# A third sorted set at the end of a four-layer kernel: batches 12 to 14 take one expert each row, batch 15 both; small constants on SP's queue

## The chip, the cores and the metric

The kernel runs on one core of a Trainium2 chip. The metric is the device time of one execution in microseconds (us), the median of several runs; less is better. The core has a matrix engine (PE, with its weight loads shown apart as PEld), a vector engine (DVE), an activation engine (ACT), a general engine (POOL), and SP, which does nothing but issue transfers. Transfers (DMAs) are issued by SP, ACT or POOL, each into a queue of its own, and carried by 16 DMA engines that all queues share. Each engine works through its own list of instructions in order.

## The reference

Sixteen batches (B = 16) of 112 rows (S) with 256 features (D), each with a context of 375 rows (SK), pass through four layers, each added to its input x. "ln" is a layer norm without weights.

```python
x = x + xattn0(ln(x), ctx)      # 16 heads of 64: q, k, v, softmax, Wo, bo
x = x + ffn0(ln(x))             # two experts, top-1, and a shared one
x = x + xattn1(ln(x), ctx)      # one head, no weights, rows masked
x = x + ffn1(ln(x))             # int8: scale from the largest |ln(x)| of ALL batches
```

The second layer matters here. Its gate gives each row to one of two experts; the other expert sees a row of zeros, so it gives the row a constant, `relu(b1) @ w2 + b2`:

```python
one_hot = one_hot(argmax(softmax(xf @ gate_w.T)), 2)
masked = xf[None] * one_hot.T[:, :, None]
h = relu(einsum('end,edh->enh', masked, w1) + b1[:, None])   # hidden 1024
routing_output = (einsum('enh,ehd->end', h, w2) + b2[:, None]).sum(0)
shared = relu(xf @ sw1 + sb1) @ sw2 + sb2
```

The fourth layer can't start before every batch has its third layer's result, since its scale is a maximum over all of them. All inputs are float32.

## The kernel before

**The stream.** The first layer is cut into 64 units (NU), four per batch, four heads each. `unit(u)` (L1055) writes out by hand what each engine does in unit u: the transposes of unit u-1's probabilities (`unit_T`, DVE, L432), scores and exponentials of unit u (L382, L399), the weighted sum of unit u-3 (L466), twelve small DMAs on SP that move blocks of transposed probabilities between partitions (`unit_move`, L444, tile pT), kT for unit u+1 (L296), the division of the probabilities by their sums on POOL in two halves (`divide`, L411), and v for unit u-2 (L317). Three more units drain it. Everything else is hung on units: `at(u, f)` puts a function at the unit's end (list `extra`), `mid(u, f)` puts it in its middle, after v and ahead of the second half of the divisions (L1090). Norms are chains of small steps that `pump` spreads between other instructions. Nothing is reordered by a scheduler: each engine's order is the program's order.

**The experts.** Batches 0 to 7 and 8 to 11 form two sorted sets (`SORTED`, L48). For each of their batches, `sort_gate` finds each row's expert (L537), `sort_place` its place in a buffer in DRAM, one expert's rows from the front and the other's from the back (L549), and `sort_put` scatters the rows there, an indirect DMA of POOL (L567). When a set is complete, `sort_counts` (L575) counts, and for each slot (128 or 112 rows, one more slot than the rows fill) gives the expert that the slot needs. SP reads that number into a register and loads this expert's weights, two tiles of 1 MB (`slot_weights`, L644, two buffers each), and the slot's rows (`slot_rows`, L649). PE then transposes the rows (`slot_turn`) and runs them through the one expert (`slot_run`, L724); `slot_store` writes the result back to DRAM (L732), and `sort_get` gathers each batch's rows from there, an indirect DMA of POOL (L738). `sort_add` adds them, with the constant of the other expert, and starts the next norm. Besides, `shared` (L715) runs the shared expert for two batches at once, and `Rows.run` is the loop of both: a first-layer step for each of 8 blocks of the hidden layer (L694) and a second-layer step behind it (L681).

Batches 12 to 15 are not sorted. The class `Experts` (L756) runs all their rows through the shared expert and both others, with a mask that zeroes the rows of expert 0: 24 steps (8 blocks by 3), for 12 and 13 together (224 columns), then for 14, then for 15 (112 columns each). Its lines are L800 (first layer) and L777 (second). The weights for it, 4 MB, are loaded by SP in units 61 and 62 (L1042 to L1044). Its steps are laid between the last units, the second attention of batches 8 to 11, and later between the second attention of 12 to 15 (L1106 to L1185).

**The third layer** per batch is `second_1` to `second_4` (L829 to L864): a transpose, scores against the transposed context (ctxT2, reloaded by `ctxT_again`), a softmax, a transpose, and the sum over the context (ctx_nat, reloaded by `load_ctx`, L103, 125 partitions by 3 by 256). `third_norm` and `third` prepare the fourth layer. For sorted batches the result goes to DRAM and comes back before the closing stage (L1154); for the others it stays in SBUF.

**The start.** SP and ACT load the weights of the first layer and the first contexts; POOL's queue loads the small constants (`row_to_all` L174, `small_const` L942, and others to L956) and fills the sorted buffers with zeros (L905). POOL adds the row bo to x (L336) before any division.

Of the kernel before, what the change touches and what calls it, by code (L numbers as in the profile page):

```python
# [47 lines left out]
SORTED = ((0, 8, 128), (8, 12, 112))  # L48
NSORT = SORTED[-1][1]


@with_exitstack
def tile_kernel(
# [120 lines left out]
    def row_to_all(src, name):  # L174
        t = const.tile([S, D], F32, tag=name, name=name)
        nc.gpsimd.dma_start(out=t, in_=src.partition_broadcast(S))
        return t
# [107 lines left out]
    def ctxT_again(b):  # L285
        if b < NSORT:
            t = ctxp.tile([P, DC, SK], F32, tag="ctxT_2", name=f"ctxT2_{b}", bufs=2)
        else:
            t = fin[0].tile([P, DC, SK], F32, tag="ctxT_2", name=f"ctxT2_{b}", bufs=B - NSORT)
        nc.sync.dma_start(out=t, in_=ctxT_d[b])  # L290
        ctxT2[b] = t
# [200 lines left out]
    def ffn_turn(b):  # L492
        g, i = divmod(b, GB)
        finish(("l1", b))
        if b >= B - GB:

            tiles = [
                fin[0].tile([P, DC, S], F32, tag=f"ffn_x{k}", name=f"ffn_x{k}_{b}", bufs=2)
                for k in range(2)
            ]  # L500
            ffn_in[b] = tiles
        else:
            if i == 0:
                group[g] = [
                    tmp.tile([P, DC, GT], F32, tag=f"ffn_x{k}", name=f"ffn_x{k}_{g}", bufs=1)
                    for k in range(1 if b < NSORT else 2)
                ]
            ffn_in[b] = [t[:, :, i * S : (i + 1) * S] for t in group[g]]
        transposed(ffn_in[b][0], normed["l1", b], f"x1_{b}")

    def gate_scores(b):
        pg = gen(f"pg_{b}")
        for dc in range(DC):
            nc.tensor.matmul(
                pg[:S, :2],
                ffn_in[b][0][:, dc, :],
                gw_sb[:, dc, :],
                start=(dc == 0),
                stop=(dc == DC - 1),
            )  # L520
# [12 lines left out]
    def ffn_turn_masked(b):  # L533
        transposed(ffn_in[b][1], masked[b], f"m1_{b}")
# [180 lines left out]
    def shared(g):  # L715

        acc = Rows(f"sh{g}", group[g][0], GB, big["sw1"], sb1_sb, big["sw2"]).run()
        sl = xall[:, g * GB : (g + 1) * GB, :]
        nc.vector.tensor_tensor(sl, acc[:S, :, :D], sl, ALU.add)
        for i in range(GB):  # L720
            b = g * GB + i
# [34 lines left out]
    class Experts:  # L756


        def __init__(self, bs, xT, m1T):
            self.bs, self.n, self.behind = bs, 0, deque()  # L760
            self.acc, self.columns = None, len(bs) * S
            self.masks = (xT, m1T)
            last = [expert_w["last", e] for e in range(2)]
            self.steps = []
            for k, (src, wa, ba, wb) in enumerate(
                (
                    (xT, big["sw1"], sb1_sb, big["sw2"]),
                    (m1T, last[1][0], b1_sb[:, 1, :], last[1][1]),
                    (xT, last[0][0], b1_sb[:, 0, :], last[0][1]),
                )  # L770
            ):
                self.steps += [(k, f, src, wa, ba, wb) for f in range(FC)]

        def second_layer(self, n, hT):
            _, f, _, _, _, wb = self.steps[n]
            for i in range(len(self.bs)):
                nc.tensor.matmul(  # L777
                    self.acc[:S, i, :D],
                    hT[:, i * S : (i + 1) * S],
                    wb[:, f, :],  # L780
                    start=(n == 0),
                    stop=(n == len(self.steps) - 1),
                )

        def run(self, count):
            name, c = self.bs[0], self.columns
            if self.acc is None:
                self.acc = ps_sc.tile([P, 2, 512], F32, tag="sc", name=f"acc_{name}")
            for _ in range(count):
                n = self.n  # L790
                if n == len(self.steps):
                    return
                k, f, src, wa, ba, wb = self.steps[n]
                if k == 2 and f == 0:

                    xT, m1T = self.masks
                    nc.gpsimd.tensor_tensor(xT, xT, m1T, ALU.subtract)
                ph = gen(f"ph_{name}_{n}")
                for dc in range(DC):
                    nc.tensor.matmul(  # L800
                        ph[:, :c],
# [5 lines left out]
                hT = tmp.tile([P, GT], F32, tag="hT", name=f"hT_{name}_{n}", bufs=3)[:, :c]  # L807
                if n % 2:
                    nc.vector.tensor_scalar(hT, ph[:, :c], ba[:, f : f + 1], 0.0, ALU.add, ALU.max)
                else:  # L810
                    nc.scalar.activation(hT, ph[:, :c], AF.Relu, bias=ba[:, f : f + 1])
                pump(1 + n % 2)
                self.behind.append((n, hT))
                if len(self.behind) > 2:
                    self.second_layer(*self.behind.popleft())
                self.n += 1

        def add(self):
            self.run(len(self.steps))
            while self.behind:  # L820
                self.second_layer(*self.behind.popleft())
            for i, b in enumerate(self.bs):
                nc.vector.tensor_tensor(xs[b], self.acc[:S, i, :D], xs[b], ALU.add)
                chain(("l2", b), norm([b], "l2"))
# [49 lines left out]
    def third(bs):  # L874

        finish(("l3", bs[0]))
        for b in bs:
            if b < NSORT:
# [15 lines left out]
    class Sorted:  # L894
        def __init__(self, first, last, slot):
# [8 lines left out]

            nc.gpsimd.dma_start(  # L905
                out=self.x.rearrange("(s p) d -> p s d", p=slot),
                in_=idle[:slot, :D].unsqueeze(1).to_broadcast([slot, self.slots, D]),
            )
# [20 lines left out]

    sorts = [Sorted(*a) for a in SORTED]  # L930
# [9 lines left out]
    x3T_d = dram.tile([NSORT, P, DC, S], F32, tag="x3T_d", name="x3T_d")  # L940

    def small_const(src, name, dtype=F32):  # L942
        t = const.tile(list(src.shape), dtype, tag=name, name=name)
        nc.gpsimd.dma_start(out=t, in_=src)
# [6 lines left out]
    nc.gpsimd.dma_start(out=b2r_sb[:2], in_=b2_rows)  # L951
    nc.gpsimd.dma_start(out=b2r_sb[2:], in_=sb2_row)
# [3 lines left out]
    nc.gpsimd.dma_start(out=wi8_sb, in_=wi8_t.rearrange("(c p) n -> p c n", p=P))  # L956
# [12 lines left out]
    for b in range(B):  # L969
# [8 lines left out]
        if b >= B - GB:  # L978
            continue
        at(u0 + UN + 3, ffn_turn, b)  # L980
        if b < NSORT:
            mid(u0 + UN + 4, sort_gate, b)
            at(u0 + UN + 4, sort_place, b)
            at(u0 + UN + 5, sort_put, b)
            continue
        mid(u0 + UN + 4, gate, b)
        at(u0 + UN + 4, ffn_turn_masked, b)
# [16 lines left out]
    at(3, load_big, "sw2", sw2)  # L1004
    for e in range(2):
# [3 lines left out]
    experts = {}  # L1009
    blocks = set()  # L1010
    for g in range(NSORT // GB):

        u = (g + 1) * GU + UN
        at(u, shared, g)
        blocks.add(u)
    for s in sorts:
        u = s.last * UN + UN
        at(u, sort_counts, s)
        u += 2
# [10 lines left out]
        for b in range(s.first, s.last):  # L1030
            mid(u - 2, sort_get, b)
            at(u, load_ctx, b, True)
# [9 lines left out]
    for j, e in enumerate((1, 0)):  # L1042
        for part in range(2):
            mid(NU - 3 + j, load_expert, ("last", e), e, part)  # L1044
# [61 lines left out]
    for u in range(NU):  # L1106
        unit(u)

    g6 = NG - 2
    b0, b1 = g6 * GB, B - GB  # L1110
    first = Experts([b0, b0 + 1], *group[g6])
    first.run(2)
    for u in range(NU, NU + 3):
        unit(u, lambda: first.run(2))
        first.run(2)
# [3 lines left out]
    for b in range(b0, B):  # L1119
        load_ctx(b, True)  # L1120
        ctxT_again(b)
# [191 lines left out]
```

## Time and profile before

| | us |
|---|---|
| Median of three runs (1113.59 to 1114.34) | 1113.76 |
| The profiled execution's own time | 1112.52 |
| Its span, first instruction to last | 1110.8 |
| PE busy in the span | 1015.4 (91%) |
| DVE, ACT, POOL busy | 522.2, 457.8, 444.2 |
| Last weighted sum of the first attention (unit 63's) starts | 986.0 |
| Last expert step ends | 1078.2 |

Span and execution time differ by 1.7 us, which lies around the first and last instruction. Times in the views are microseconds from the span's start. "L466" is a line of the kernel. In a view by lines or in a timeline, "out<-in xN" gives the tiles written and read and the number of instructions; what stands in brackets is how long the engine was idle before and what ended it. "SPq" and the like are an engine's instruction queue, for SP its DMA issues. "PEclk" is the clock that the throttle granted to PE as a share of the full one. "DMA" is the mean busy share of the 16 DMA engines.

The profile shows an almost always busy PE with two kinds of exceptions: the first 40 us, and about 910 to 958 us, the last units. The closing stage after 1078.2 is a chain of latencies (batch 15's third layer, the global maximum, and the quantized product of all batches).

### The profile page before, as it was taken

The page shows a single profiled execution, that of the slowest core. Times are in us where ns is not written, and L with a number is a line of the kernel's source. Part 1 is how long each engine was busy: PE and PEld are TensorE (multiplying, and loading weights), DVE is VectorE, ACT ScalarE, POOL GpSimd, SP SyncE. Part 2 cuts the span into 40 slices and gives each one's busy share as a digit, 9 for nine tenths or more (in the row PEclk, how much of TensorE's full clock was granted, in tenths as well). Part 3 has the DMA queues.
Part 4 walks back from the last instruction along what each step waited for, and adds up shares of the span by engine and source line. Part 5 has one row for each costly group of instructions (what it writes and reads, how often), then busy time and mean ns, then how long its engine had stood idle before and what let it go on. Part 6 is the DMA issues. An engine that isn't in the chain of part 4 may idle for free. (4 is left out here: it accounts for less than half of the span.)

```text
span 1110.8 us, 17703 instructions
## 1 busy us (share of the span) xinstructions
PE 1015.4 (91%) x6021; PEld 772.1 (70%) x6021; DVE 522.2 (47%) x1304; ACT 457.8 (41%) x1241; POOL 444.2 (40%) x479
## 2 busy tenths in 40 slices
PE   7899999999999999999999997988889977799995
PEld 4576677767777776877768774676667755588774
DVE  3647535554463554344342346536535345333324
ACT  2664535653553465343441435335333444112212
POOL 5654534552544455232330326535322436113113
PEclk9899999999999999999999999989999998799997
DMA  9663312231231223175563423425645416424002
GB/s 278 164 172 94 80 39 70 74 85 34 79 88 45 64 75 84 28 205 148 159 200 101 130 66 103 124 64 144 176 127 149 147 40 210 120 81 129 1 1 67
DMA packets 142850, 117.83 MB, mean 106 GB/s; under 512 B 15190, under 2 KB 133288, under 8 KB 142760
## 3 DMA queue, kind: packets, MB, share of 16 engines
q1 hardware_dynamic: 131848, 102.51, 33.0%
q10 hardware_dynamic: 8960, 9.39, 3.0%
q0 software_dynamic: 1952, 4.81, 1.4%
q8 instruction: 48, 0.79, 0.3%
q14 instruction: 42, 0.34, 0.1%
HBM read 64.92 MB, written 13.98 MB: 71 GB/s over the span
## 5 line engine op out<-in xcount | busy, mean ns | idle before, releaser
L411 POOL TENSOR_SCALAR p<-p,rden 128x375 f32<-128x375 f32 x256 | 316.6, 1250 | 331.0 <-DVE rden L408 326.0
L399 ACT ACTIVATE p<-sc,nmax 128x375 f32<-128x375 f32 x256 | 143.2, 570 | 258.5 <-DVE nmax L390 250.1
L296 PE MATMUL pk<-ctxT,wk 128*128 128x375 f32 x512 | 195.4, 505 | 8.6 <-ACT v L328 4.0
L317 PE MATMUL pv<-wv,ctxT 128*128 128x256 f32 (+1 forms) x768 | 190.3, 384 | 7.3 <-ACT v L328 6.2
L317 PEld LDWEIGHTS pv<-wv,ctxT 128*128 128x128 f32 (+1 forms) x768 | 143.9, 189 | 59.0 <-ACT v L328 11.4
L432 DVE STREAM_TRANSPOSE blk<-p 128x384 f32<-128x384 f32 x256 | 131.7, 551 | 20.8 <-POOL p L411 17.5
L454 ACT COPY pT<-blk 32x384 f32<-32x384 f32 x256 | 130.0, 508 | 16.2 <-DVE rden L408 11.8
L296 PEld LDWEIGHTS pk<-ctxT,wk 128*128 128x128 f32 x512 | 91.8, 194 | 63.7 <-issue 13.2
L382 PE MATMUL sc<-kT,qT 64*128 64x375 f32 x512 | 103.2, 518 | 11.8 <-ACT kT L305 9.8
L390 DVE TENSOR_REDUCE nmax<-sc 128x2 f32<-128x750 f32 x128 | 112.2, 913 | 3.6 <-PE sc L382 3.5
L466 PEld LDWEIGHTS pa<-pT,v 128*64 128x64 f32 (+1 forms) x1536 | 75.7, 138 | 35.1 <-issue 18.9
L330 DVE COPY v<-pv 119x256 f32<-119x256 f32 x64 | 26.9, 421 | 144.9 <-PE pv L317 143.5
L466 PE MATMUL pa<-pT,v 128*64 128x112 f32 (+1 forms) x1536 | 90.5, 266 | 4.0 <-DVE v L330 4.0
L237 POOL TENSOR_SCALAR var_l<-mv_l 112x1 f32<-112x1 f32 (+1 forms) x56 | 13.1, 233 | 166.4 <-DVE mv_l L234 139.9
L382 PEld LDWEIGHTS sc<-kT,qT 64*128 64x128 f32 x512 | 44.5, 190 | 46.2 <-ACT kT L305 14.3
L305 ACT COPY kT<-pk 128x375 f32<-128x375 f32 x128 | 61.4, 480 | 16.7 <-PE pk L296 16.1
L486 PE MATMUL po<-wo,oT 128*112 128x256 f32 x256 | 59.6, 387 | 1.3 <-ACT v L328 1.3
L353 PE MATMUL pq<-xT,wq 128*128 128x224 f32 x256 | 54.9, 357 | 4.5 <-ACT v L328 3.9
L486 PEld LDWEIGHTS po<-wo,oT 128*112 128x112 f32 x256 | 46.4, 182 | 12.7 <-ACT v L328 2.2
L353 PEld LDWEIGHTS pq<-xT,wq 128*128 128x128 f32 x256 | 46.7, 190 | 7.9 <-ACT v L328 6.0
L399 ACT ACTIVATION_READ_ACCUMULATOR p<-sc,nmax 128x1 f32 x256 | 51.7, 202 | 0.0
L845 ACT ACTIVATE e<-e,nmax 112x375 f32<-112x375 f32 x16 | 9.7, 607 | 98.0 <-DVE nmax L843 93.1
(212 smaller groups left out, 1336.9 us busy)
## 6 DMA issues: line engine op xcount, KB each, us to landing
pT<-blk SPq DMA_DIRECT2D x768, 48.0 KB
ctx<-in_ctx SPq DMA_DIRECT2D x31, 375.0 KB
ctxT_d<-ctxT SPq DMA_DIRECT2D x16, 375.0 KB
ctxT<-ctxT_d SPq DMA_DIRECT2D x16, 375.0 KB
sw<-in_sw ACTq DMA_DIRECT2D x2, 1024.0 KB
ew<-in_w ACTq DMA_DIRECT2D x2, 1024.0 KB
out<-y SPq DMA_DIRECT2D x8, 224.0 KB
x<-in_x ACTq DMA_DIRECT2D x1, 1344.0 KB
```

The source lines that it names most:

```text
L296: nc.tensor.matmul(pk[:, :SK], wk_sb[:, dc, m * P : (m + 1) * P], ctxT[b][:, dc, :], start=(dc == 0), stop=(dc == DC - 1),)
L305: nc.scalar.copy(t, pk[:, :SK])
L317: nc.tensor.matmul(pv[: KP[c], n * UD : (n + 1) * UD], ctxT[b][:, dc, c * P : c * P + KP[c]], wv_sb[:, dc, k * UD : (k + 1) * UD], start=( ...
L353: nc.tensor.matmul(pq[:, :GT], wq_sb[:, dc, m * P : (m + 1) * P], xT0[g][:, dc, :], start=(dc == 0), stop=(dc == DC - 1),)
L382: nc.tensor.matmul(sc[:, j, :SK], qT[g, m][r, i * P : (i + 1) * P], kT[b, m][r, :], start=True, stop=True,)
L390: nc.vector.tensor_reduce(nmax, sc[:, :, :SK], AX.X, ALU.max, negate=True)
L399: nc.scalar.activation(p[:, :SK], sc[:, j, :SK], AF.Exp, bias=nmax[:, j : j + 1], accum_out=den[:, j : j + 1])
L411: nc.gpsimd.tensor_scalar(p, p, rden[:, j : j + 1], None, ALU.mult)
L432: nc.vector.transpose(blocked[u][:, :, h * 32 : (h + 1) * 32], probs[u][h].rearrange("p (n k) -> p n k", k=32),)
L454: nc.scalar.copy(pT[r, :, i, :], of[r, :, i, :])
L466: nc.tensor.matmul(pa[j * DH : (j + 1) * DH, j2 * S : (j2 + 1) * S].rearrange("p (i q) -> p i q", q=QB), vv[b, k][: KP[c], c, h * DH : (h ...
L486: nc.tensor.matmul(po[:S, :D], oT[b][:, m, :], big["wo"][:, m, :], start=(m == 0), stop=(m == MC - 1))
```

## The change

- `SORTED` gets a third set, batches 12 to 14 with slots of 112 rows (4 slots). `NBODY` = 12 is the end of the first two sets and takes `NSORT`'s place where buffers of the closing stage are chosen.
- The shared expert of 12 and 13 runs in unit 60, that of 14 in unit 64 (`shared` takes a list of batches).
- The third set's weights and rows are loaded by SP from units 65 and 66 on, its four slots run after the last unit, mixed with the steps of batch 15, which alone still takes both experts (`LastExperts`). The context tiles of 12 to 15 are issued after slot 3's weights, expert 1's weights for batch 15 after slot 2, expert 0's after slot 3. Then come the three gathers and the second attention of 12, 13 and 14 between the remaining steps.
- For all sets: `sort_get` moves from the middle of its unit to the end, and `load_ctx` one unit earlier.
- The small constants, bo, bias and the closing stage's scale row come on SP's queue, and the zero fill of the sorted buffers is issued by SP in unit 1 (`Sorted.clear`).

```diff
-SORTED = ((0, 8, 128), (8, 12, 112))
+SORTED = ((0, 8, 128), (8, 12, 112), (12, 15, 112))
 NSORT = SORTED[-1][1]
+NBODY = SORTED[-2][1]
...
     def row_to_all(src, name):
-        nc.gpsimd.dma_start(out=t, in_=src.partition_broadcast(S))
+        nc.sync.dma_start(out=t, in_=src.partition_broadcast(S))
...
-    def shared(g):
+    def shared(bs):
+        g, i = divmod(bs[0], GB)
+        n = len(bs)
+        src = group[g][:, :, i * S : (i + n) * S]
+        acc = Rows(f"sh{bs[0]}", src, n, big["sw1"], sb1_sb, big["sw2"]).run()
...
+        def clear(self):
+            nc.sync.dma_start(
+                out=self.x.rearrange("(s p) d -> p s d", p=self.slot),
+                in_=idle[: self.slot, :D].unsqueeze(1).to_broadcast([self.slot, self.slots, D]),
+            )
...
     def small_const(src, name, dtype=F32):
-        nc.gpsimd.dma_start(out=t, in_=src)
+        nc.sync.dma_start(out=t, in_=src)
...
+    for s in sorts:
+        at(1, s.clear)
...
-    for g in range(NSORT // GB):
+    for g in range(NG - 1):
         u = (g + 1) * GU + UN
-        at(u, shared, g)
+        at(u, shared, [g * GB, g * GB + 1])
+    at(NU, shared, [NSORT - 1])
     for s in sorts:
         u = s.last * UN + UN
         at(u, sort_counts, s)
+        if s.last > NBODY:
+            continue
...
-            mid(u - 2, sort_get, b)
-            at(u, load_ctx, b, True)
+            at(u - 2, sort_get, b)
+            at(u - 1, load_ctx, b, True)
...
-    for j, e in enumerate((1, 0)):
-        for part in range(2):
-            mid(NU - 3 + j, load_expert, ("last", e), e, part)
+    tail = sorts[-1]
+    mid(NU + 1, slot_weights, tail, 0, 0)
+    at(NU + 1, slot_weights, tail, 0, 1)
+    mid(NU + 2, slot_weights, tail, 1, 0)
+    at(NU + 2, slot_weights, tail, 1, 1)
+    at(NU + 1, slot_rows, tail, 0)
+    at(NU + 2, slot_rows, tail, 1)
...
+    last = LastExperts(b)           # b = 15
+    slot_turn(tail, 0)
+    ffn_turn(b)
+    slot_run(tail, 0)
+    slot_store(tail, 0)
+    slot_weights(tail, 2, 0)
+    slot_weights(tail, 2, 1)
+    slot_rows(tail, 2)
+    slot_turn(tail, 1)
+    gate(b)
+    some_rest()
+    slot_run(tail, 1)
+    slot_store(tail, 1)
+    slot_weights(tail, 3, 0)
+    slot_weights(tail, 3, 1)
+    slot_rows(tail, 3)
+    for c in range(NBODY, B):
+        load_ctx(c, True)
+        ctxT_again(c)
...
+    last.run(4)
+    last.masked = ffn_turn_masked(b)
+    slot_turn(tail, 2)
+    last.run(4)
+    slot_run(tail, 2)
+    slot_store(tail, 2)
+    load_expert(("last", 1), 1, 0)
+    load_expert(("last", 1), 1, 1)
+    slot_turn(tail, 3)
+    some_rest()
+    slot_run(tail, 3)
+    slot_store(tail, 3)
+    load_expert(("last", 0), 0, 0)
+    load_expert(("last", 0), 0, 1)
+    for c in range(tail.first, tail.last):
+        sort_get(c)
...
+    last.run(3)
+    for c in range(tail.first, tail.last):
+        sort_add(c)
+    c0, c1, c2 = range(tail.first, tail.last)
+    for f in (
+        lambda: second_1(c0),
+        lambda: (second_2(c0), second_1(c1)),
+        lambda: second_3(c0),
+        lambda: (second_4(c0), third_norm([c0]), second_2(c1)),
+        lambda: (second_3(c1), second_1(c2)),
+        lambda: (second_4(c1), third_norm([c1]), second_2(c2)),
+        lambda: (second_3(c2), third([c0])),
+        lambda: (second_4(c2), third_norm([c2])),
+        lambda: third([c1]),
+    ):
+        last.run(1)
+        f()
+    last.run(3)
+    third([c2])
+    last.add()
```

`LastExperts` is `Experts` for batch 15 alone: the same 24 steps of 112 columns, each taking its weights when it comes to them.

## The prediction

> **What bounds the kernel now.** I read the page's busy shares first (PE 91%), then the sums by stretch from where the change begins to bite, then each engine's timeline around what PE waited for. Stretches (us, busy and count for PE, PEld, DVE, ACT, POOL, then PE clock, DMA share, GB/s):
>
> ```profile
> PE 1015.4 (91%) x6021; PEld 772.1 (70%) x6021; DVE 522.2 (47%) x1304; ACT 457.8 (41%) x1241; POOL 444.2 (40%) x479
> 909.77:932.10 22.33, 16.03 (x76) 10.84 (x75) 11.00 (x28) 9.04 (x22) 17.16 (x17) 0.77 0.55 165
> 932.10:951.14 19.04, 6.14 (x50) 4.56 (x50) 7.63 (x19) 6.10 (x17) 7.72 (x9) 0.79 0.62 192
> 951.14:1019.80 68.66, 68.64 (x379) 57.53 (x380) 25.42 (x68) 13.29 (x34) 14.00 (x24) 0.96 0.38 115
> 1019.80:1078.20 58.40, 54.69 (x344) 46.99 (x343) 20.60 (x61) 13.44 (x39) 8.21 (x17) 0.97 0.00 1
> ```
>
> From 951 to 1078 PE sets the pace: less matmul there is less time. Between 909.8 and 951.1 PE stands still, and the timelines of POOL, SP and PE say for whom:
>
> ```profile
> 662.64 1.07 POOL L740 DMA_INDIRECT got<-y_s,place  x1 [8.08 <-DMA y_s<-yrow]
> 909.64 1.05 POOL L740 DMA_INDIRECT got<-y_s,place  x1 [8.35 <-PE pk L296]
> 916.97 1.62 PE L382 MATMUL sc<-kT,qT 64*128 64x375 f32 x4 [6.30 <-ACT kT L305]
> 938.28 0.47 SPq L640 DMA_DIRECT2D ew_('last', 0)_8369<-in_w  x1
> 938.79 0.52 SPq L105 DMA_DIRECT2D ctx<-in_ctx  x1
> 951.14 2.87 PE L855 MATMUL pa<-ctx,pT_l 125*112 125x256 f32 x6 [12.90 <-DMA ctx<-in_ctx]
> ```
>
> POOL stood 8 us before each set's first gather (sort_get), with the second half of a unit's divisions behind it. PE stood 12.9 us for a context tile issued behind 2 MB of last-expert weights. Prices of one expert step (first layer, second layer) from the chain in order of time, for 224 and for 112 columns:
>
> ```profile
> 976.95 0.86 PE acc L777 x4
> 977.82 0.76 PE ph L800 x4
> 1022.23 0.43 PE acc L777 x2
> 1022.66 0.43 PE ph L800 x4
> ```
>
> So 1.62 and 0.86 us. Last, what the queue carries when it holds context tiles, and what held the first divisions:
>
> ```profile
> DMA packets 1417, 1.64 MB, mean 137 GB/s; under 512 B 45, under 2 KB 1297, under 8 KB 1416
> DMA packets 2036, 3.01 MB, mean 182 GB/s; under 512 B 125, under 2 KB 1499, under 8 KB 2036
> DMA packets 1534, 2.48 MB, mean 355 GB/s; under 512 B 58, under 2 KB 1172, under 8 KB 1534
> 22.59 0.76 POOL L956 DMA_DIRECT2D wi<-in_wi_t  x1 [1.88 <-DMA x_s<-idle]
> 23.38 4.91 POOL L411 TENSOR_SCALAR p<-p,rden 128x375 f32<-128x375 f32 x4
> ```
>
> These are 970.5-982.5 (context tiles), 996-1012.5 (context and transposed context) and 871.5-878.5 (slot weights).
>
> [...]DMA share near a third and 113 GB/s for most of 970.5-982.5 against 355 for weights on 128 partitions. [...]the six matmuls at 951.14 took 2.87 us, at 966.00 1.46.
>
> **The change, part by part** (sums against the profiled run: span 1110.8, its time 1112.52).
>
> *Start.* Nine small loads and three fills of the sorted buffers leave POOL's queue for SP's. POOL loses their issue (about 0.55-1 us each) and the 4.2 and 1.9 us waits before the last ones. But the row bo now stands behind 2.9 MB on SP's queue (two x pairs, context tiles 0 and 1, wk, wv), and POOL's first add needs it, with the iotas and all divisions behind. That queue moved 2.70 MB in the first 20 us while the fills took 1.64 MB beside it, so I put bo's landing at 20-23 us. Adds 1.41 and some ten small operations 1.1: first division at 22.5-25.5 instead of 23.38. The fills (2.1 MB, 6-9 us at 220-350 GB/s) now stand between two units' pT moves; those are needed only at 54.45, but that cover is thin: 0 to +3. The nine small issues cost SP some 5 us (0.35-0.6 each), hidden while SP has nothing to send between 17.7 and 29.1; without that cover they would add to the first pT moves. Together -1 to +5, taken +1.
>
> *Body.* sort_get moves from before the unit's second divisions to the unit's end. At 662: the second division starts at 654.6 instead of 663.8. The gather still issues at 662.6, and the next unit's first division follows it at 663.7 instead of 666.99; the norm's chain gains 4.5 us (bounds 0, -5.5). The seven later gathers no longer stand between two divisions: up to 1.05 each where DVE waits for POOL's norm, which it does 20 times in the run; taken -3 of -7.4. Context loads issue one unit earlier: the 1.99 us wait at 800.86 mostly goes, -1.5. They take buffers that were read two units before, so SP doesn't stand for one. Sum -9 (0 to -14).
>
> *From 892 on.* Batches 12-13 did 24 wide steps; 16 go (25.9 us). Their slots with batch 14's come to 32 narrow steps where 14 had 16 for its experts: +16 narrow, 13.8. Net -12.1; four slot transposes and three sort_place pairs for three masked transposes, +1. Slots are 336/112+1 = 4 whatever the tokens choose. shared of 12-13 (8 x 1.62 = 13 us) now sits in unit 60, and the 4 MB of last-expert weights leave units 61-62: the stalls 6.3 and 12.9 and their half-clock stretches (5.4, from sc, pa and pk at 917-923 and pa, pe at 951-956 against their usual times) go: -24.6. The old tail's own idle and half clock (3.7+1.6) go with its order, -5.3.
>
> sort_gate, sort_place and sort_put of 12-14 stand where gate and the masked turn stood: three DVE operations of 0.2 us and one gather-like issue of 1.04 on POOL for one of 0.93, both beside PE's matmuls; uncovered they would cost 0.7 a batch.
>
> New waits, walked in the old clock by adding PE's work unit by unit (weighted 1.31, scores 1.46, kT 2.73, v 2.58, attention_out 3.45, the second attention's pe 1.27 and pa 1.30): unit 60 ends at 914, 61 at 922, 62 at 936, 63 at 945, 64 with shared of batch 14 (6.9) at 960, 65 at 967, 66 at 974. The pT moves keep up (7.7 us of issue a unit, each landed 7 us or more before its use). SP reads the tail's index at 962.5 when DVE has the counts, needs 1.0 us for the read (as at 784.5), and slots 0's and 1's weights land by 972 and 979. Where the walk is too short: in unit 62 batch 8's normed rows stand in DVE ahead of the block transposes and wait for POOL's norm behind four divisions, and exps, kT and v queue behind that, +3. Slot 0 is turned at 974, but batch 15's norm (po ends 972.8) holds PE, +1.7. Slots 0 and 1 end at 991. SP then issues slot 3's weights (6 us at 355 GB/s, data from about 995), then eight context loads (3.1 MB; 2.67 MB of that kind took 16.5 us, so 19), then slot 2's store, then expert 1's weights for batch 15: first half at about 1022.6, second at 1026. PE has eight steps, slots 2 and 3 (7.0 each) and is done at 1013.8: it waits 8.5+3.5 = 12. Slot 3's store lands behind those weights at 1026.5; gather 1.05 (3.1 to landing) and norm 3 give 1033, another 4.8. Batches 13 and 14 then come through one DVE chain: 3.6+1+1. Half clock after these, +2. Sum +29.1. From 892.35 to the last acc at 1078.2: 185.9-12.1+1-24.6-5.3+29.1 = 174. From there 32.6 us of closing work stay as they are. So -12.
>
> Sum 1-9-12 = -20: span 1091, run 1092.5; against the median of the runs, 1.2 above the profiled one, 1094.
>
> **Rivals.** *The queue keeps pace* (0.21): [...]PE waits only for store, gather and norm (1013.8+0.5+2.8+3.1+3 = 1023): 1083. For: two kinds of load reached 300 GB/s and more in moments of 996-1012. Against: the mean there was 182. *Thin gain* (0.17): bo and the fills cost 5-6, the body gives the first 4.5 only: 1104. *Slower* (0.08): the tail's queue becomes the bound. 7.1 MB stand between 995 and 1027 in the walk, 222 GB/s; each lost us moves the end. It decides at 54 us, 131 GB/s, what context tiles alone got at 970 (137): then 1116 or more. Against: 4 of the 7.1 MB are weights at 355. A balance within 0.2% of the median (what a measurement tells from no change), 0.04.
>
> **Numbers.** Forecast 0.50, own range 1086-1102. Below 1077 about 0.06, above 1111 about 0.13: range 1077-1111. Faster 0.21+0.50+0.17 = 0.88, same 0.04, slower 0.08.
>
> **What would show it.** No POOL wait near 8 us before the first gather of the first two sets; no ctx wait at the end of the attention stream; a PE gap of 15-20 us after slot 3, waited for expert 1's weights, then the gathered rows; first divisions at 22-26 us. Wrong if the gap is absent or over 35 us, or if units 2-5 lose more than 5 us to late pT moves.

## The result, and the profile after

The changed kernel takes 1123.78 us (median of 7 runs, 1117.90 to 1125.48) against 1113.31 for the kernel before, measured beside it (7 runs, 1109.23 to 1114.34). The ratio is 1.0091, 95% interval 1.0064 to 1.0117: the change costs about 10 us, where the prediction had a gain of 20. The profiled execution, the slowest of the seven, has a span of 1123.6 us, 12.8 longer than before.

The span split at four points that both traces have (unit 5's scores, unit 47's, unit 60's, and the end of the last expert step), with the prediction's share beside it:

| stretch, us | before | after | difference | predicted |
|---|---|---|---|---|
| start to unit 5's scores | 63.4 | 72.5 | +9.1 | +1 |
| to unit 47's scores | 584.4 | 587.5 | +3.0 | 0 |
| to unit 60's scores | 245.9 | 232.6 | -13.2 | -9 |
| to the last expert step's end | 184.5 | 198.9 | +14.4 | -12 |
| closing stage | 32.6 | 32.1 | -0.5 | 0 |

PE's busy time in all, from the page:

```profile
PE 1015.6 (90%) x6003; PEld 769.3 (68%) x6003; DVE 530.2 (47%) x1329; ACT 458.4 (41%) x1242; POOL 437.8 (39%) x471
```

The stretches of the tail (us, then busy time and count of PE, PEld, DVE, ACT, POOL, then PE clock, DMA share, GB/s):

```profile
892.60:937.55 44.95, 42.79 (x228) 31.52 (x227) 21.56 (x52) 18.70 (x50) 20.95 (x21) 1.00 0.27 64
937.55:987.33 49.78, 43.69 (x276) 34.39 (x275) 27.01 (x75) 14.71 (x39) 14.96 (x22) 0.90 0.55 160
987.33:1034.20 46.87, 42.85 (x259) 35.19 (x257) 11.61 (x39) 9.82 (x28) 4.73 (x8) 0.96 0.65 200
1034.20:1053.51 19.31, 5.97 (x24) 5.05 (x24) 3.08 (x10) 0.71 (x2) 3.72 (x5) 0.69 0.91 290
1053.51:1091.49 37.98, 28.17 (x127) 21.30 (x128) 14.49 (x41) 7.19 (x20) 6.71 (x14) 0.84 0.00 1
1091.49:1123.60 32.11, 19.27 (x119) 14.50 (x117) 15.05 (x32) 8.62 (x16) 9.83 (x11) 0.84 0.20 58
```

The rows are: unit 60 to unit 63's scores; the draining units; the four slots with eight steps of batch 15 between; the wait behind slot 3; the second attentions of batches 12 to 14 with the rest of batch 15's steps; the closing stage. PE's busy time is the same as before to 0.2 us. The 18 matrix instructions fewer, and the narrower ones, show nowhere in it: PE ran at a lower clock where it was not fed (0.69 in the fourth row, 0.84 in the fifth), and waited. In the fourth row it is busy for 6.0 of 19.3 us.

The timelines of POOL, SP and PE at the places that the prediction named (start, duration, engine, what; in brackets the idle time before and what ended it):

```profile
20.88 1.41 POOL L337 TENSOR_TENSOR x<-x,bo 112x256 f32<-112x256 f32 x2 [14.05 <-DMA bo<-in_bo]
23.32 4.91 POOL L412 TENSOR_SCALAR p<-p,rden 128x375 f32<-128x375 f32 x4
39.77 2.53 SPq L908 DMA_DIRECT2D x_s<-idle  x3
42.40 14.63 SPq L445 DMA_DIRECT2D pT<-blk  x12
62.18 2.51 PE L467 MATMUL pa<-pT,v 128*64 128x112 f32 x24 [8.13 <-DMA pT<-blk]
674.74 1.06 POOL L734 DMA_INDIRECT got<-y_s,place  x1 [5.60 <-DMA y_s<-yrow]
945.96 0.64 PE L260 MATMUL pt_x<-ident,xn_l 112*128 112x112 f32 x2 [2.27 <-ACT v L329]
960.57 1.20 PE L686 MATMUL ph_sh<-ffn_x,sw 128*128 128x112 f32 x4 [2.49 <-DVE v L331]
1021.90 0.69 PE L673 MATMUL acc_sl<-ew_(12, 2)_9037,hT_sl 128*112 128x256 f32 x2 [0.45 <-ACT hT_sl L698]
1040.16 1.19 PE L781 MATMUL ph_last<-ffn_m,ew_('last', 1)_9271 128*128 128x112 f32 x4 [5.97 <-DMA ew_('last', 1)_9271<-in_w]
1053.51 0.64 PE L260 MATMUL pt_x<-ident,xn_l 112*128 112x112 f32 x2 [7.38 <-DVE xn_l L249]
```

The row bo lands at 20.9 and the first division comes at 23.3, as predicted. But the fills go out at 39.8, ahead of unit 1's pT moves. Those then need 14.6 us to be issued; the last piece is there at 62.2, and PE has waited 8.1 us for it. The kernel before issued 24 moves in 18.6 us, and PE did not wait:

```profile
29.11 18.56 SPq L444 DMA_DIRECT2D pT<-blk  x24
54.45 1.38 PE L466 MATMUL pa<-pT,v 128*64 128x112 f32 x24
```

The first gather of the first set now stands behind the divisions, and its wait of 5.6 us costs nothing. The two old stalls, 6.3 us for kT and 12.9 us for a context tile, are gone. In their place stand many smaller waits (945.96 and 960.57 are the largest before the slots), and behind slot 3 the 6.0 us for expert 1's weights and the 7.4 us for batch 12's gathered and normed rows.

### The profile page after: what moved, and what is told of

Same layout as the page of the kernel before. It is cut to its first block, busy times and chain, and to the rows that moved or that the text cites. A ratio compares the mean times of both kernels' runs of the same rounds, so it can differ in the third digit from the quotient of the medians.

```text
span 1123.6 us, 17744 instructions
## 1 busy us (share of the span) xinstructions
PE 1015.6 (90%) x6003; PEld 769.3 (68%) x6003; DVE 530.2 (47%) x1329; ACT 458.4 (41%) x1242; POOL 437.8 (39%) x471
## 4 chain that ended last, share of the span: by engine, by line
PE 26%; DVE 7%; DMA 6%; ACT 5%; SPq 4%; issue 2%; POOL 1%; DVEq 0%; ACTq 0%; POOLq 0%
PE acc_sl L673 4%; PE ph_sl L686 4%; SPq L445 3%; PE acc_sh L673 2%; PE ph_sh L686 2%; PE pv L318 2%; ACT pT L455 2%; ACT p L400 2%; PE po L487 2%; DVE blk L433 2%; PE pa L836 1%; PE pa L467 1%; PE pk L297 1%; DVE nmax L391 1%; DMA ew_(8, 1)_7131<-in_w 1%
## 5 line engine op out<-in xcount | busy, mean ns | idle before, releaser
L297 PEld LDWEIGHTS pk<-ctxT,wk 128*128 128x128 f32 x512 | 91.5, 194 | 62.9 <-issue 12.8
L306 ACT COPY kT<-pk 128x375 f32<-128x375 f32 x128 | 61.5, 481 | 12.2 <-PE pk L297 11.6
L673 PE MATMUL acc_sh<-sw,hT_sh 128*112 128x256 f32 x240 | 61.0, 385 | 0.0
L696 DVE TENSOR_SCALAR hT_sl<-ph_sl,slot_b 128x112 f32<-128x112 f32 (+1 forms) x68 | 23.1, 340 | 79.7 <-PE ph_sl L686 64.3
L686 PE MATMUL ph_sh<-ffn_x,sw 128*128 128x224 f32 (+1 forms) x256 | 55.8, 352 | 3.6 <-DVE v L331 2.5
L698 ACT ACTIVATE hT_sl<-ph_sl,slot_b 128x112 f32<-128x112 f32 (+1 forms) x68 | 24.3, 360 | 83.5 <-PE ph_sl L686 66.8
```

What stands on the lines that cost most here:

```text
L297: nc.tensor.matmul(pk[:, :SK], wk_sb[:, dc, m * P : (m + 1) * P], ctxT[b][:, dc, :], start=(dc == 0), stop=(dc == DC - 1),)
L673: nc.tensor.matmul(self.acc[:n, i, :D], hT[:, i * n : (i + 1) * n], self.wb[:, f, :], start=(f == 0), stop=(f == FC - 1),)
L686: nc.tensor.matmul(ph[:, : self.n], self.wa[:, dc, f * P : (f + 1) * P], self.src[:, dc, :], start=(dc == 0), stop=(dc == DC - 1),)
```

## The experiments

Each ratio is to the kernel before, measured beside it on the same chip. Where two kernels are compared, the difference of their ratios is multiplied by 1113.5 us; with the intervals given, such a difference is uncertain by 3 to 5 us. The changed kernel stands at 1.0091.

**The parts of the change, each alone.** First the start:

```diff
 (kernel before)
-        nc.gpsimd.dma_start(out=t, in_=src...)      # small constants, bo, bias
+        nc.sync.dma_start(out=t, in_=src...)
...
+    for s in sorts:
+        at(1, s.clear)                              # fills, on SP's queue
```

> The kernel before, with the start's edits alone: the small constants and bo on SP's queue, and the fills of its two sorted buffers (1.75 MB) there at the end of unit 1. Theory (the fills hold up the pT moves of units 1 and 2 and nothing else is lost): unit 4's scores start 8 to 10 us later, first divisions stay within 0.3 us of 23.4, time up by 8 to 10 us. Rival (the 10 us needed the third buffer's fill, 0.46 MB, or another part of the change beside it): up by less than 4.

Measured: 1.0099 (1.0069 to 1.0130), 11 us slower, a little more than expected. PE's wait for unit 1's pT is 7.5 us. (The times that this expectation and the next give for unit 4's scores are those of DVE's first maximum over them, which stands behind the late work; the scores themselves start between 50.6 and 51.9 in all these traces. The two fills are 1.6 MB.) The other way round, the changed kernel with its fills elsewhere:

```diff
-    for s in sorts:
-        at(1, s.clear)
+    for u, s in zip((6, 20, 22), sorts):
+        at(u, s.clear)
```

> The changed kernel, with the three zero fills of the sorted buffers at the ends of units 6, 20 and 22 on SP's queue, instead of all at the end of unit 1. Theory (the fills stand ahead of the pT moves of units 1 and 2, and PE's 8.1 us wait at 62 us is their doing): the wait goes, unit 4's scores start near 53.3 us as before the change instead of 63.2, and the time falls by 8 to 10 us, to about 1114. Rival (the moves are late because the shared expert's weights on ACT's queue, 2 MB at 47 to 60 us, take the DMA engines, or because the small loads keep SP): less than 3 us.

Measured: 0.9971 (0.9958 to 0.9983), 13.4 us less than the changed kernel. SP's issues and PE's weighted sum of unit 1 in this trace:

```profile
29.81 18.75 SPq L445 DMA_DIRECT2D pT<-blk  x24
54.21 1.38 PE L467 MATMUL pa<-pT,v 128*64 128x112 f32 x24
```

Moves at 0.78 us each, and no wait. So the place of the fills is the whole cost of the start; the small constants on SP's queue cost nothing that shows. The gain is larger than the 8 to 10 us expected; the profiled run gives 6.9 of it (its own time, 1118.57, is the slowest of the 20), so the rest isn't accounted for.

Next the body's two edits on the kernel before, together and each alone:

```diff
-            mid(u - 2, sort_get, b)
-            at(u, load_ctx, b, True)
+            at(u - 2, sort_get, b)
+            at(u - 1, load_ctx, b, True)
```

> The kernel before, with the body's two edits alone: the gathers at the end of the unit instead of ahead of the second half of the divisions, and the context loads one unit earlier. Theory (they are what took 13.2 us out of units 47 to 57 in the changed kernel): units 47 to 57 shorter by 11 to 14 us, time 1113.3 less 8 to 13, 1100 to 1105; up to 4 us are given back at the end, where the gathers of batches 10 and 11 come half a unit later. Rival (most of the 13 us comes from the late start's shift of DMA and clock, not from these edits): gain below 6 us.

> The kernel before, with the second loads of the context tiles one unit earlier and nothing else. Theory (the 12.9 us stall at 951 is a context load's place behind the last experts' weights and twelve pT moves; one unit earlier it stands ahead of them): the stall and its half clock go, 12 to 16 us, and up to 4 us of units 52 to 57; 1097 to 1101 against 1113. Rival (the stall moves to the next load or to the weights): gain below 6.

> The kernel before, with the gathers at the units' ends and nothing else. Theory (POOL's 8 us waits for the first gather of each set go, with the second divisions that stood behind them): 9 to 11 us out of units 47 to 57, the 6.3 us stall at 917 partly, the 12.9 us stall at 951 stays; 1100 to 1106. The prediction's share for it: 7.5 us. Rival (the body's 13 us come from the context loads): gain below 4.

Measured: together 0.9774 (0.9747 to 0.9801), 1087.54 us, 25 us faster; context loads alone 0.9901 (0.9874 to 0.9928), 1102.96 us, just short of what was expected; gathers alone 0.9890 (0.9854 to 0.9926), 1101.76 us, as expected. The expectation for both was half of what came: 13.1 us between units 47 and 57 as foreseen, and instead of a loss at the end another 16 between unit 60 and the last expert step. PE's waits over 4 us in the last two, from the timelines; the first two lines are of the gathers alone, the other two of the context loads alone:

```profile
799.38 2.87 PE L855 MATMUL pa<-ctx,pT_l 125*112 125x256 f32 x6 [8.01 <-DMA ctx<-in_ctx]
941.62 2.87 PE L855 MATMUL pa<-ctx,pT_l 125*112 125x256 f32 x6 [8.47 <-DMA ctx<-in_ctx]
```

```profile
911.31 1.62 PE L382 MATMUL sc<-kT,qT 64*128 64x375 f32 x4 [5.86 <-ACT kT L305]
954.14 2.81 PE L837 MATMUL pe<-ctxT,xT 128*112 128x375 f32 x4 [4.68 <-DMA ctxT<-ctxT_d]
```

With the gathers alone the units before 799 are 9 us shorter, and then the context tile, no sooner there than before, takes 8.0 of them back (it had cost 2.0). The stall of 12.9 at the end shrinks to 8.5 only. With the context loads alone, that stall is gone and the one for kT stays. Each edit lays the other's stall bare; together neither is left. In the stretch of units 47 to 57 the context loads are worth 3.7 us alone, the gathers 3.3, and both 13.1. Over the whole kernel this interplay does not stand out of the noise: 11.0 and 12.2 us alone, 25.2 together.

Last the third sorted set alone, that is the changed kernel with start and body put back:

```diff
-    for s in sorts:                            # fills and constants on POOL's queue again
-        at(1, s.clear)
...
-            at(u - 2, sort_get, b)
-            at(u - 1, load_ctx, b, True)
+            mid(u - 2, sort_get, b)
+            at(u, load_ctx, b, True)
```

> The third sorted set alone: the changed kernel, with the constants and fills back on POOL's queue at the start, the gathers ahead of the second divisions, and the context loads at their old units. Theory (the set saves at most 12 us of PE's work, and costs more in waits between units 62 and the last expert step, where the kernel before had expert steps to lay between): slower than before by 8 to 18 us, 1122 to 1132. The prediction's sum for this part was a gain of 12, 1101. Rival (third set and body edits interact so that the set only pays without them): 1113 or less.

Measured: 1.0135 (1.0106 to 1.0164), 15 us slower. So the three parts are +11, -25 and +15. They add to +1 and not to the change's +10: the body edits' gain at the end can't be had beside the third set, which has already removed those two stalls in its own way, and the gathers' new place costs something there (below).

**What the third set does to PE.** From unit 60's scores to the last expert step, in the kernel before, with the body edits alone, and after:

```profile
893.66:1078.20 184.54, 161.16 (x931) 130.42 (x930) 72.70 (x192) 50.55 (x137) 50.59 (x70) 0.93 0.29 87
```

```profile
883.16:1051.71 168.55, 156.03 (x929) 126.19 (x928) 73.30 (x192) 50.25 (x137) 50.24 (x70) 0.99 0.32 95
```

```profile
892.60:1091.49 198.89, 163.47 (x911) 127.44 (x910) 77.75 (x214) 51.12 (x139) 51.08 (x70) 0.91 0.44 130
```

With the body edits alone PE idles 12.5 us of this stretch at nearly full clock; after the change 35.4 us, and its work, 12 us smaller by the prices of the steps, takes 7.4 us longer. That is 30 us between them: 23 of waiting, and 7 because PE's work, at a lower mean clock (0.91 against 0.99), took longer by more than the narrow steps saved. Five runs take the waits apart, each an edit of the changed kernel.

*The draining units.* The shared expert of 12 and 13 taken from unit 60, two steps at a time into the middle of units 63 to 66; and the gathers of 10 and 11 ahead of the second divisions again:

```diff
-    for g in range(NG - 1):
+    for g in range(NG - 2):
...
+    fill = Filler([NBODY, NBODY + 1])          # shared expert in pieces
+    for u in (NU - 1, NU, NU + 1, NU + 2):
+        mid(u, fill.some, 2)
```

```diff
-            at(u - 2, sort_get, b)
+            (mid if u - 2 >= NU - 2 else at)(u - 2, sort_get, b)
```

> The changed kernel, with the shared expert of batches 12 and 13 (8 wide steps, 13 us of PE) taken from unit 60 and laid two steps at a time into the middle of units 63 to 66. Theory (the kernel before filled PE's waits in the draining units with expert steps; without them PE waits there for norms, gathers and copies, and falls to half clock): of the 49.8 us from unit 63's scores to slot 0's transpose some 6 are waits and 4.5 half clock; with the filler this stretch grows by 3 to 8 us instead of 13, and the time falls by 5 to 10. Rival (the waits are for chains that the filler only delays): stretch grows by 13, time unchanged within 2.

> The changed kernel, with the gathers of batches 10 and 11 ahead of the second half of the divisions of units 62 and 63, where the kernel before had them, instead of at the units' ends. Theory (in the short last units half a unit is too little for a gather of 6.5 us: DVE waits 4.1 us for gathered rows between 937 and 987, with PE's copies behind it): 2 to 4 us less. Rival (DVE has slack there): within 1 us.

Measured: 1.0047 (1.0035 to 1.0059), 4.9 us less, and 1.0040 (1.0024 to 1.0057), 5.7 us less. The filler's gain is just under what was expected: it brings a wait of its own, 2.6 us in the first piece for hT, since two steps at a time leave PE standing for the activation. The gathers' place is worth more than expected. What helps in the long units of the body harms in the short ones of this drain.

*Slots 2 and 3* took 1.12 us a step where slots 0 and 1 took 0.87 (the wait at 1021.90 above):

```diff
     last.run(4)
+    while last.behind:
+        last.second_layer(*last.behind.popleft())
     slot_run(tail, 2)
```

> The changed kernel, with the last expert's two pending second-layer steps issued ahead of slot 2, so that they no longer hold two of the three hT buffers while slots 2 and 3 run. Theory (slots 2 and 3 take 1.12 us a step instead of 0.87 because a single hT buffer is left): their steps go back to 0.87, slots 2 and 3 end 4 to 5 us earlier. By the queue theory (PE then waits for expert 1's weights all the same) the wait of 6.0 us behind slot 3 grows by as much, and the time falls by 0 to 2 us only. If steps and waits are independent it falls by 4 to 5. Rival (the steps are slow because of the 243 GB/s of transfers beside them): steps stay at 1.12, time unchanged.

```profile
1037.82 2.90 PE L781 MATMUL ph_last<-ffn_m,ew_('last', 1)_9273 128*128 128x112 f32 x12 [9.73 <-DMA ew_('last', 1)_9273<-in_w]
```

Measured: 1.0069 (1.0044 to 1.0095), 2.4 us less, which is within the noise. The steps are back at 0.87, so their cause was the buffers: three hT buffers, two of them held by batch 15's pending steps. PE got most of it back as waiting, 9.7 us for the weights instead of 6.0.

*The queue behind slot 3.* The eight context loads were first moved as they are, then cut as they stand:

```diff
     slot_rows(tail, 3)
-    for c in range(NBODY, B):                  # moved up, ahead of slot_turn(tail, 0)
-        load_ctx(c, True)
-        ctxT_again(c)
```

> The changed kernel, with the eight loads of context and transposed context of batches 12 to 15 issued ahead of slot 0, where SP's queue stands empty from 983 to 999 us, instead of behind slot 3's weights. Queue theory (they hold up expert 1's weights for batch 15, and slot 3's store behind these): the 6.0 us wait for the weights goes, slot 3's result lands 4 to 7 us earlier, the first transpose of batch 12's second attention comes near 1046 instead of 1053.5, time lower by 5 to 8 us. Rival (the chain store, gather, norm sets the end whatever the queue): less than 2 us.

```profile
1017.69 0.60 PE L651 MATMUL pt_s<-ident,row 112*128 112x112 f32 x2 [10.40 <-DMA row<-x_s]
```

Measured: 1.0138 (1.0115 to 1.0161), 5.2 us slower: a miss. SP was at these loads from 981.6 to 1001.1, so slot 0's store and slot 2's weights came 2 to 3 us late and slot 2's rows 9 us, and PE waited 10.4 us for the rows. The queue had looked empty from 983 to 999, but the gap was smaller than what was put into it.

The cut, for these four loads of 125 partitions only:

```diff
-        nc.sync.dma_start(out=t, in_=view)
+        nc.sync.dma_start(out=t[:112], in_=view[:112])
+        nc.sync.dma_start(out=t[112:], in_=view[112:])     # 13 partitions
```

> The changed kernel, with each of the four context loads behind slot 3 cut in two transfers, of 112 and of 13 partitions, in the same place of SP's queue. Theory ([...]the eight loads hold the queue from 1009.7 to 1027.8 us): the queue is through by about 1020, expert 1's weights are issued when slot 2 frees their buffer, near 1024, and are there when slot 3 ends; PE's 6.0 us wait goes, slot 3's result lands 6 us earlier; time lower by 5 to 8 us. Rival (the queue is slow for another reason, so that the earlier place of these loads, which gained nothing, and their shape are both beside the point): less than 2 us.

The transfers from the first of the eight loads to slot 2's store behind them (each time the busy share of the 16 DMA engines in 40 slices, in tenths, then the sums), whole (1009.7 to 1027.8 in the changed kernel) and cut (1005.8 to 1020.1):

```profile
DMA  8977989999999999665468993333339789533333
DMA packets 2851, 4.25 MB, mean 235 GB/s; under 512 B 103, under 2 KB 2264, under 8 KB 2850
```

```profile
DMA  6979999899999999999999999999999899999999
DMA packets 3131, 4.51 MB, mean 315 GB/s; under 512 B 180, under 2 KB 2510, under 8 KB 3131
```

```profile
1043.08 0.64 PE L265 MATMUL pt_x<-ident,xn_l 112*128 112x112 f32 x2 [9.48 <-DVE xn_l L254]
```

Measured: 1.0020 (0.9998 to 1.0041), 7.9 us less, at the top of the expectation. The wait for the weights is gone; the next one, for batch 12's rows, has grown from 7.4 to 9.5 us. How one transfer is spread over the engines the traces do not show; they show the busy share. Whole, there are long stretches with three tenths of the engines busy, at 113 to 140 GB/s; cut, nine tenths nearly throughout, and a mean of 315 GB/s against 235. That the cut helps is measured, then; why these loads leave the engines idle is not. In the body the same cut (of the loads of units 48 and on, on top of the two body edits) gains nothing that shows:

> The kernel before with the body's two edits alone, and in addition every second load of a context tile cut in two transfers, of 112 and of 13 partitions. Theory ([...]): lower than the body edits alone (1087.5) by 2 to 6 us. Rival (they are hidden in the body, and each costs SP one more issue of 0.6 us): 1087 to 1089.

Measured: 0.9752 (0.9722 to 0.9783) against 0.9774 without the cut, the intervals overlap: the rival.

**Together, and what stays.** All five edits (fills, filler, gathers, flush, cut loads):

> The changed kernel with five mends at once: zero fills at units 6, 20 and 22; the last expert's pending steps issued ahead of slot 2; the four late context loads in two parts each; the shared expert of batches 12 and 13 laid into units 63 to 66; the gathers of batches 10 and 11 in mid-unit. Theory (five separate causes): the gains alone, 13.2, 2.4, 7.9, 4.9 and 5.7 us, add up to 34; the flush's 4 us come free now that the weights no longer bind, the fillers' two overlap in part: 1088 to 1096. Rival (the waits at the end lie one behind another, so that a shortened one only uncovers the next): 1100 to 1106. In either case it doesn't fall clearly below the body edits alone (1087.5), if the third set itself gains nothing.

Measured: 0.9921 (0.9890 to 0.9952), 1102.64 us. The gains alone add to 34 us, together they are 19, as the rival had it. Of the large waits at the end, the one for batch 12's rows is still 7.5 us in this trace. Two runs on top of the five edits (the first needs no flush, since no steps of batch 15 are pending then):

```diff
-    last.run(4)                                # both ahead of slot 2
-    last.run(4)
...
-    last.run(3)
+    last.run(8 + 3)                            # behind slot 3
```

> The kernel with the five mends, and in addition the shared expert's 8 steps of batch 15 (7 us of PE) moved from ahead of slot 2 to behind slot 3. Queue theory (expert 1's weights are issued at 1008.5 behind the context loads, whatever PE does; slot 3's store lands behind them): slots 2 and 3 end 7 us earlier, the steps fill what were waits, but the gathers start at most 2 us earlier; 1 to 3 us less than the 1102.6 of the five mends. Rival (PE's own order sets the end): 5 to 7 us less.

```diff
-            t, None, sort_of[b].y, bass...
+            t, None, (sorts[1] if b >= NBODY else sort_of[b]).y, bass...
```

> The kernel with the five mends, but batches 12 to 14 gather their rows from the second set's results, which have long been complete: the expert part of these three batches is another one's, so that the chain slot 3, store, gather is cut while all work stays. Theory (this chain holds PE idle behind slot 3): the 7.5 us wait before batch 12's second attention goes, with some half clock behind it; 7 to 10 us less than the 1102.6 of the five mends, 1092 to 1096; still above the body edits alone (1087.5), since the three second attentions then stand one behind another with few steps between. Rival (PE waits for the last weights in any case): less than 3.

```profile
1026.72 0.64 PE L265 MATMUL pt_x<-ident,xn_l 112*128 112x112 f32 x2 [2.60 <-DVE xn_l L254]
```

Measured: 0.9909 (0.9873 to 0.9945), no difference, as the queue theory had it; and 0.9864 (0.9830 to 0.9897), 4 us less by the medians and 6 by the ratios, less than expected. With free gathers the wait before batch 12's second attention falls from 7.5 to 2.6 us, but the last weights still come late (2.8 us), and from that transpose to the end of the steps it takes 38 us as with every order that was tried. That pass is three second attentions, one behind the other through single DVE and POOL norms, with 12 to 14 narrow steps between them, at a clock of 0.84 in the changed kernel. It stands behind the slots because it needs their results. No run takes it apart, so what is left of the third set's loss after the five edits stays unexplained in part.

Last, the body edits with the gathers of the late units put back:

```diff
-            at(u - 2, sort_get, b)
+            (mid if u - 2 >= NU - 3 else at)(u - 2, sort_get, b)
```

> The kernel before with the body's two edits, but with the gathers from unit 61 on (batches 9 to 11) ahead of the second divisions as before. Theory (with the body edits alone DVE stands 8.5 us for gathered rows between 882 and 960, PE 3.7 and 2.6 behind it): lower than the body edits alone (1087.5) by 2 to 5 us. Rival (the division that the gather then delays costs as much): 1086 to 1089.

Measured: 0.9796 (0.9767 to 0.9824), no better than 0.9774: the rival. Without the third set, then, the place of the late gathers gains nothing; the 5.7 us above belong to the changed kernel's drain. The body edits alone beat both kernels, by 25 us and by 35.

## Why the prediction was wrong

**Start: the term for the zero fills, 0 to +3.** It was sized by the data alone, 6 to 9 us, against slack until 54.45. What stands behind the fills was left out. The first three of unit 1's moves took 1.3 to 2.0 us each to issue, where each of the others took 0.6. Then SP stood 2.9 us before the eighth. The wait view of SP's queue (total, times, longest) names ACT's first load of the shared expert, issued at 42.6, as what that move waited for, until 53.9:

```profile
SPq L445 <- DMA sw<-in_sw: 2.9, 1, 2.9
```

And the last moves fall beside ACT's second load (1 MB, issued at 54.81): from 55.8 to 58.6 us, 0.58 MB of ACT's queue moved and 0.05 MB of SP's. So the moves were there at 62 instead of 54. The prediction said that the cover was thin and did not price what happens without it: +9 to +11. With the fills elsewhere all of this goes, though ACT's loads keep their places. bo, first division and the small issues were right. (Two of the three fills leave POOL's queue; the third is new.)

**Units 5 to 47: not foreseen, +3.** Two stretches in units 40 and 44 ran at a lower clock, 1.7 us each (see the end). The change didn't bring that about: in the eighteen traces of this case units 40 to 47 take 144.4 to 144.6 us with none of these drops, 145.9 to 146.5 with one and 147.7 to 147.9 with both, and the trace of the body edits alone has both, too.

**Body: -9 foreseen, -13.2 measured.** The first gather gave 4.7 us in units 48 and 49, as worked out (4.5). The later gathers gave another 4.9 up to unit 54, where 3 was taken, and units 55 to 57 3.6, where the context wait had been booked with 1.5. That last term was priced apart from the first: the context wait of 2.0 us was what was left of it behind slower units; with faster ones it would have been 8.0.

**From 892 on: -12 foreseen, +14 measured.** The removed terms hold. PE's step prices were right (0.87 and 1.62), and both stalls went. But 13 to 16 us of the 24.6 booked for them need no third set, since the body edits alone bring the same. The failed step is the last, "New waits, walked in the old clock by adding PE's work unit by unit": +29.1, where the same sum that gives the measured 198.9 needs about 55. By stretches of that walk, from unit 60's weighted sum (892.35 before, 891.29 after):

| to | walk | measured | what the runs show |
|---|---|---|---|
| unit 63's scores | 43.7 | 46.3 | |
| slot 0's transpose | 38 | 49.8 | waits of the drain: no steps to lay between (4.9 back with a filler), gathers half a unit too late (5.7) |
| end of slots 0 and 1 | 17 | 18.9 | |
| end of slot 3 | 22.8 | 28.0 | one hT buffer: 1.12 us a step |
| batch 12's second attention | 19.2 | 19.3 | |
| last expert step | 33.4 (the rest of the walk's 174) | 38.0 | low clock (0.84) between the three attentions |

The walk added PE's work where PE no longer sets the pace. The kernel before kept it busy there with expert steps; the change takes these away, and what remains in the drain waits for norms, gathers and copies (6.1 us of idle time between 937.6 and 987.3, at a clock of 0.90). It is this exchange, PE's work against its cover, that was not priced: for the drain the walk had waits of 4.7 us (+3 and +1.7). The gap behind slot 3, where it looked for waits most closely, came out to 0.1 us by luck, of other parts: 6.0 us for weights instead of 12, and more for gathers and norm. That the queue of context loads holds it was right (7.9 us when cut).

**The rivals.** The only one on the slower side had the tail's queue as the bound, below 131 GB/s. The queue ran at 235 and is 8 us of the loss. The time came out on that rival's side for other reasons.

**The signs named ahead**: no 8 us wait of POOL before a first gather (5.6 us, with no division behind it), no context wait at the end of the stream, and first divisions at 22 to 26 were there. The gap of 15 to 20 us was there as a stretch of 19.3 us, 13.4 of it waiting, for the weights and then the rows. The one that was named as refuting, units 2 to 5 losing more than 5 us to late moves, was there as well, and was the start's loss. None of the signs looked at the drain.

## What to carry to other kernels

Work that an edit removes from the bottleneck engine may be what covered the latencies around it; before booking it as a gain, list what that engine will wait for in its place, stretch by stretch. Price two moved waits together, since removing one lets the other show its whole length. And ask of every transfer that is put into a queue not only when its own data is needed but what stands behind it, and at what rate it runs (here 235 GB/s with the context loads whole, 315 with them cut).

## What the runs showed of the hardware

The clock of PE dropped in one trace and not in the other behind the same wait in the same unit (44). PE's timeline before and after the change:

```profile
582.71 1.53 PE L296 MATMUL pk<-ctxT,wk 128*128 128x375 f32 x4 [1.91 <-ACT v L328]
```

```profile
593.20 1.84 PE L297 MATMUL pk<-ctxT,wk 128*128 128x375 f32 x4 [1.92 <-ACT v L329]
```

In both traces all changes of the clock lie a whole number of steps of 3.41 us apart. The steps round this wait, before and after (PE's busy time is the second number, its clock the third from the end):

```profile
578.08:581.49 3.41, 2.71 (x18) 2.15 (x16) 2.12 (x9) 3.39 (x11) 2.24 (x2) 1.00 0.62 196
581.49:584.90 3.41, 2.19 (x8) 1.58 (x9) 0.00 (x0) 2.37 (x7) 2.63 (x3) 1.00 0.31 77
```

```profile
590.87:594.28 3.41, 1.50 (x8) 0.88 (x7) 0.71 (x4) 2.99 (x8) 3.41 (x4) 1.00 0.36 72
594.28:597.69 3.41, 3.41 (x13) 2.66 (x12) 0.71 (x3) 0.47 (x1) 0.33 (x1) 0.50 0.27 53
```

In the kernel before, the border of two steps (581.49) cuts the wait in two; PE is busy for 2.71 and 2.19 us of them, and the clock stays. After the change the whole wait lies in one step, behind a few small matmuls; PE is busy for 1.50 us of it, and the next step runs at half clock, which costs 1.7 us: from the start of this kT to the start of the next q product it is 4.57 us (593.20 to 597.77) instead of 2.90 (582.71 to 585.61). Over the whole of both traces, each of the 20 steps at full clock in which PE was busy for 1.64 us or less was followed by one at half clock. Of the nine with 1.67 to 1.95 us three were (1.71, 1.86 and 1.95), and of those with more none. That is a count in two traces; no run was made to take the clock apart.

SP's issues themselves took longer in two places of the changed kernel: the three moves right behind the fills 1.3 to 2.0 us, the other moves of unit 1 0.6. Between the 125-partition loads each transposed context load took 3.5 to 4.1 us to issue; with those loads cut, 0.35 us (SP then stood between the issues, 2.9 us at most).
